# Moving the rank product of the expert routing from between the query parts to behind the second chunk's scores and first values

## The chip, the cores and the metric

The kernel runs on one core of one Trainium2 chip. The metric is the time of the whole kernel on the device in microseconds, the median of several executions. The engines of the core are called by the profile's names: PE (TensorE, matrix products), PEld (its weight loads), DVE (VectorE), ACT (ScalarE), POOL (GpSimd) and SP (SyncE, which issues most DMAs). Each engine works through its own instructions in program order and waits on semaphores of the others.

## The reference: what is computed

One transformer block on x of 8 batches x 2048 tokens x 256 features, all in float32.

```
h = layernorm(x) * (1 + ca) + sa
x = x + ga * attention(h)          # linear attention with decay, 16 heads of 64
h = layernorm(x) * (1 + cb) + sb
x = x + gb * experts(h)            # 8 experts of 256x256, the best 2 for each token
```

Attention: q and k pass through elu + 1, a decay a = sigmoid(h Wa + ba + 2) per head and token multiplies the running state S and the running key sum z, and the output of a token is q S / (q z). Experts: scores by a 256x8 product, softmax, the two best experts with weights of at least 0.1, scaled to sum to one; the output is half of the weighted sum of the two experts' products.

## The kernel before

**Tiling.** The tokens are cut into 64 groups of 256 tokens (8 groups for each batch), and each group into two chunks of 128 tokens. One pass of the main loop (variable n, -2 to 64) works on several groups at once, as a pipeline written out by hand: `here` is group n, whose attention is computed chunk by chunk (objects c0 and c1); `prev` is group n-1, whose attention is done and which is normalised again and routed to experts; `ahead` is group n+1, whose keys, queries and key sums are made; `coming` is group n+2, whose normalised rows are turned and whose decays are made. Expert products of an earlier batch (tiles of 128 rows, `expert_tiles`) are strewn among these steps.

**Order.** The order of the instructions on each engine is the order of the Python statements (`manual_schedule`); nothing reorders them later. Steps that belong to different groups are Python generators, and `advance(gen)` issues the next part of one.

**The routing.** `routing(prev, unit)` (called `rt` in the loop) has six parts, parted by `yield`. Part 1: the gate product and the scores (L642 to L670). Part 2: softmax and the best expert (L672 to L687). Part 3: the second best, `both` (which experts each token uses, L704) and the running count of tokens per expert `hist` (L709, L713). Part 4, the one that is moved: two PE products into the PSUM tile `prank` (L719 with the triangular matrix `before`, L722 with `ones`) give each token its rank among the tokens of its expert; then four DVE instructions make row numbers of it: L729 adds the first row of the expert's list (`rmark`), L734 multiplies the choices with it (`rpicks`), L735 sums them into `places`, and L737 casts them to the integer tile `rrows`. Part 5: four scatters on POOL's queue (L770, a memset of one element, and L771, an indirect DMA that writes 128 rows of `prev` to the lists in DRAM at the rows in `rrows`). Part 6: the weights (`weigh`, L659 to L662 on DVE). Each of the parts 1 to 6 is issued by one `advance(rt)` in a pass.

The last two groups (62 and 63) are not routed through lists (`DenseUnit`): for them part 4 issues nothing. So part 4 works in 62 passes, n = 1 to 62, and in all of them `here` exists.

**Around the old place of part 4.** `qp = project(ahead.hT, "q", ...)` makes the queries in four parts. A part is 8 matmuls on PE into a tile `pq` (L340), two activations on ACT into `lowq` (L350, L351; two buffers) and one DVE instruction that writes `qT` (L352). After each part, POOL multiplies the key sums by it (`times_queries`, L1177). Part 4 of the routing stands behind the second part's `times_queries(1)` and ahead of the third part of the queries: on PE its products lie between the second and the third `pq`, and on DVE its four instructions lie between the second and the third `qT`.

**Around the new place.** After the queries come, for the second chunk of `here`: `c1.scores(0)` (L506 on PE, two products by DVE, L515), `c1.keys()` (transposes L525 on PE, DVE writes `kd`, L528; not for the last group of a batch), `c1.scores(1)` (L506, L515), and `c1.values(0)` (4 matmuls `pv` on PE, L542, a copy on ACT, L549). Then come part 5, the scatters; `expert_tiles` (L884 turns a tile's rows into `pxt`, L900 multiplies them into `py`, L904 on DVE adds the bias into `yg`); the statistics of another group's rows (L283, L284); `denominators` (PE sums `pd`, L463, from what POOL's L1177 left; DVE makes the reciprocal `rd`, L471 and L472, which goes out to DRAM and comes back spread as `rb`); `c1.values(1)`; part 6 of the routing; `decayed_queries` (POOL, L1062); and the second chunk's outputs (`po`, L562 and L579 on PE; DVE's L591 multiplies them by `rb`).

**PSUM.** Tiles of 2 KB rotate through two rings of four. The ring "mm" holds `pq`, `pk`, `pv`, `pxt`, `py` and `pw`; the ring "big" holds the scores `sc` (four in a chunk), `po`, `ps`, the small tiles of the routing (`prank` among them) and `pd`. A tile can be written when the tile four places before it in its ring has been read.

Of the kernel before, what the change touches and what calls it, by code (L numbers as in the profile page):

```python
# [30 lines left out]
def adaln_block_kernel(  # L31
# [1019 lines left out]
    def advance(gen, k=1):  # L1051

        for _ in range(k):
            if gen is not None:
                next(gen, None)
# [66 lines left out]
    def expert_tiles(k=1, look=True):  # L1122
        while queue and not queue[0].unit.dense and on_chip() < AHEAD:
            load_tile()
        if queue and not loaded:
            load_tile()
        for i in range(k):

            while loaded and len(turned) < (2 if look or i + 1 < k else 1):
                t = loaded.pop(0)  # L1130
                t.turn()
                turned.append(t)
            if turned:
                now = turned.pop(0)
                now.apply()
                load_tile()
                left[now.unit.n] -= 1
                if left[now.unit.n] == 0:
                    u = now.unit
                    waiting.extend(Combine(u, g) for g in range(u.first, u.end))  # L1140
                    if u.dense:
                        u.finish()
# [30 lines left out]
    def times_queries(jj):  # L1173

        if ahead:
            part = slice(2 * jj, 2 * jj + 2)
            nc.gpsimd.tensor_mul(zz[:, part, :], zz[:, part, :], ahead.qT[:, part, :])  # L1177

    c0 = plan = planned = None
    for n in range(-2, total + 1):  # L1180
        here, ahead, coming = live.get(n), live.get(n + 1), live.get(n + 2)
# [79 lines left out]
        if prev:  # L1261
# [21 lines left out]
            rt = routing(prev, unit)  # L1283
# [37 lines left out]
        times_queries(0)  # L1321
        advance(qp)
        times_queries(1)
        advance(rt)
        advance(qp)
        keep_sums(slice(4, 8))
        times_queries(2)
# [13 lines left out]
        if here:  # L1341
            c1.scores(0)
            c1.keys()
            c1.scores(1)
        if here:
            c1.values(0)
        advance(rt)
        expert_tiles(share[3])
        advance(dk)
# [110 lines left out]
```

## Time and profile before

| what | value |
|---|---|
| median of 3 executions | 3779.65 us (3770.18 to 3783.37) |
| the profiled execution, its own time | 3800.69 us |
| its span, first to last instruction | 3799.0 us |
| mean granted TensorE clock | 0.974 |
| PE busy | 3545.7 us, 93% of the span |
| DVE busy | 2756.5 us, 73% |
| ACT busy | 2073.6 us, 55% |
| POOL busy | 1891.9 us, 50% |
| part 4's DVE instruction L734, 62 times | 1280 / 1293 / 2054 ns (min / median / max) |

Most passes of the main loop take 50 to 62 us, some of the last ones up to 75 us (by the starts of part 4 in successive passes). A busy share is an average over stages with different limits: which engine sets the pace of a stage is read from the chain of waits and from who waits for whom in that stage.

### The profile page before, as it was taken

The numbers are of one execution on the slowest core, as the hardware profiler recorded it, in microseconds if no ns is written. First come the engines' busy times: TensorE is split into PE (matmuls) and PEld (weight loads), VectorE is DVE, ScalarE is ACT, GpSimd is POOL, SyncE is SP. The second block draws the span as 40 slices with busy tenths as digits, with TensorE's granted clock in tenths as the row PEclk, the third lists the DMA queues.
The fourth block names the chain that finished last, engine by engine and source line by source line (L and its number), as shares of the span: only waits on it lengthen the run. The fifth ranks groups of instructions, "written<-read, shape, count | busy, mean of one in ns | idle before, by whom it ended". The sixth has DMA issues, their size and how long they took to land.

```text
span 3799.0 us, 82207 instructions
## 1 busy us (share of the span) xinstructions
PE 3545.7 (93%) x28998; PEld 2724.2 (72%) x28998; DVE 2756.5 (73%) x6395; ACT 2073.6 (55%) x5295; POOL 1891.9 (50%) x2114
## 2 busy tenths in 40 slices
PE   8999999999999999999999999999999999989876
PEld 6777767777677777777777777777767777767664
DVE  5777788777767777677768668767677677767655
ACT  5555556655555555555546555556555556555532
POOL 2444444343655455454654456454464454555654
PEclk9999999999999999999999999999999999999987
DMA  6555556675676567676575675775775766787866
GB/s 168 142 152 144 141 167 181 185 203 158 192 215 179 179 189 211 177 215 173 173 230 161 200 209 166 206 209 162 200 209 172 202 180 177 216 227 214 229 198 190
DMA packets 347406, 712.11 MB, mean 187 GB/s; under 512 B 43736, under 2 KB 212968, under 8 KB 322416
## 3 DMA queue, kind: packets, MB, share of 16 engines
q1 hardware_dynamic: 318880, 631.29, 59.2%
q0 software_dynamic: 27264, 74.49, 5.8%
q8 instruction: 229, 3.75, 0.4%
q14 instruction: 185, 1.52, 0.1%
q10 hardware_dynamic: 848, 1.07, 0.1%
HBM read 577.29 MB, written 132.53 MB: 187 GB/s over the span
## 4 chain that ended last, share of the span: by engine, by line
PE 62%; DVE 18%; DMA 7%; issue 7%; ACT 3%; POOL 1%; SPq 1%; another core or an unknown queue 0%; DVEq 0%; POOLq 0%
PE pk L340 9%; PE pw L629 9%; PE pv L542 8%; PE py L900 6%; PE po L579 6%; PE pq L340 5%; DVE at L447 5%; PE sc L506 3%; PE ps L613 3%; PE po L562 3%; DVE qT L352 2%; DMA xg<-xrows 2%; PE pxt L884 2%; DVE dec L515 2%; PE pd L463 2%
## 5 line engine op out<-in xcount | busy, mean ns | idle before, releaser
L429 ACT ACTIVATE dec<-dec,lt 128x128 f32<-128x128 f32 x2048 | 629.7, 390 | 20.5 <-POOL dec L423 20.5
L1177 POOL TENSOR_TENSOR at<-at,qT 128x512 f32<-128x512 f32 x256 | 342.2, 1349 | 422.0 <-DVE qT L352 341.0
L340 PE MATMUL pk<-hT_a,wk_sb 128*128 128x256 f32 x2048 | 516.0, 398 | 1.9 <-issue 1.9
L542 PE MATMUL pv<-wv_sb,hT_a 128*128 128x512 f32 x1024 | 486.1, 607 | 11.2 <-DVE qT L352 11.2
L340 PE MATMUL pq<-hT_a,wq_sb 128*128 128x256 f32 x2048 | 489.7, 388 | 1.9 <-DVE yg L904 1.3
L889 ACT ACTIVATE xgT<-pxt,modT,modT 128x128 f32<-128x128 f32 x622 | 249.0, 453 | 427.5 <-PE pxt L884 412.0
L629 PE MATMUL pw<-wo_sb,oT 128*128 128x256 f32 x2048 | 474.6, 385 | 6.4 <-DMA xt<-in_L_attn_x_dram 5.9
L629 PEld LDWEIGHTS pw<-wo_sb,oT 128*128 128x128 f32 x2048 | 389.8, 194 | 60.6 <-DVE oT L591 8.3
L340 PEld LDWEIGHTS pk<-hT_a,wk_sb 128*128 128x128 f32 x2048 | 384.8, 197 | 67.1 <-issue 7.6
L340 PEld LDWEIGHTS pq<-hT_a,wq_sb 128*128 128x128 f32 x2048 | 381.4, 191 | 56.6 <-DVE kT L352 1.7
L447 DVE TENSOR_TENSOR_SCAN at<-at,z,kT 128x256 f32<-128x256 f32 x448 | 396.8, 925 | 2.0
L591 DVE TENSOR_TENSOR oT<-po,rb 128x512 f32<-128x512 f32 x256 | 168.0, 684 | 314.0 <-DMA rb<-rdd 90.0
L423 POOL TENSOR_SCALAR_AFFINE_SELECT dec<-dec 128x2048 f32<-128x2048 f32 x128 | 258.7, 2021 | 273.3 <-DMA dec<-led 218.1
L579 PE MATMUL po<-dec,v 128*64 128x128 f32 x4096 | 299.3, 280 | 68.7 <-issue 63.3
L900 PE MATMUL py<-we,xgT 128*128 128x256 f32 x1244 | 341.4, 399 | 20.6 <-DVE kT L352 8.5
L515 DVE TENSOR_TENSOR dec<-sc,dec 128x512 f32<-128x512 f32 x512 | 326.8, 680 | 42.3 <-PE sc L506 40.0
L542 PEld LDWEIGHTS pv<-wv_sb,hT_a 128*128 128x128 f32 x1024 | 182.9, 190 | 204.7 <-issue 150.6
L579 PEld LDWEIGHTS po<-dec,v 128*64 128x64 f32 x4096 | 235.3, 138 | 127.5 <-issue 109.0
L634 POOL TENSOR_TENSOR xt<-xt,dx 128x256 f32<-128x256 f32 x128 | 93.8, 733 | 446.7 <-DVE dx L633 444.9
L506 PE MATMUL sc<-qT,kT 64*128 64x128 f32 x4096 | 297.3, 285 | 0.0
L506 PEld LDWEIGHTS sc<-qT,kT 64*128 64x128 f32 x4096 | 249.7, 188 | 62.9 <-issue 62.9
L1062 POOL TENSOR_TENSOR el<-el,qT 128x1024 f32<-128x1024 f32 x120 | 285.8, 2381 | 5.6 <-POOL whole L1070 0.2
(198 smaller groups left out, 6155.8 us busy)
## 6 DMA issues: line engine op xcount, KB each, us to landing
dec<-led SPq DMA_DIRECT2D x128, 1024.0 KB
we<-ew_d SPq DMA_DIRECT2D x311, 384.0 KB
at<-ad SPq DMA_DIRECT2D x128, 512.0 KB
el<-led SPq DMA_DIRECT2D x256, 256.0 KB
rb<-rdd SPq DMA_DIRECT2D x128, 512.0 KB
xg<-xrows SPq DMA_DIRECT2D x311, 128.0 KB
yrows<-yg SPq DMA_DIRECT2D x311, 128.0 KB
xt<-in_L_attn_x_dram SPq DMA_DIRECT2D x64, 256.0 KB
```

The source lines that it names most:

```text
L340: nc.tensor.matmul(pp[:, j * GT : (j + 1) * GT], w[:, k, (jj + j) * P : (jj + j + 1) * P], hT[:, k, :], start=(k == 0), stop=(k == KD - 1),)
L423: nc.gpsimd.affine_select(out=dec, in_=dec, compare_op=ALU.is_ge, fill=1e30, base=0, pattern=[[0, H], [1, C]], channel_multiplier=-1,)
L429: nc.scalar.activation(dec[:, h, :], dec[:, h, :], AF.Exp, scale=-1.0, bias=x.lt[:, 0, ch, h : h + 1])
L447: nc.vector.tensor_tensor_scan(zz[:, j, :], at[:, j, :], kT[:, j, :], 0.0 if z is None else z[:, j : j + 1], ALU.mult, ALU.add,)
L506: nc.tensor.matmul(sc[q][:, i, :], self.kT[rows, half * 4 + i, self.tok], self.qT[rows, half * 4 + i, self.tok], start=True, stop=True,)
L515: nc.vector.tensor_mul(w4, sc[q], w4)
L542: nc.tensor.matmul(pv, self.hT[:, k, self.tok], wv_sb[:, k, i * 512 : (i + 1) * 512], start=(k == 0), stop=(k == KD - 1),)
L579: nc.tensor.matmul(po[half * DH : (half + 1) * DH, i, :], self.v[:, h * DH : (h + 1) * DH], self.dec[:, q * NP + j, :], start=(self.S is N ...
L629: nc.tensor.matmul(pw[:, :D], self.oT[:, j, :], wo_sb[:, j, :], start=(j == 0), stop=(j == NP - 1))
L900: nc.tensor.matmul(py[:, :D], self.xT[:, k, :], self.w[:, k, :], start=(k == 0), stop=(k == KD - 1))
L1062: nc.gpsimd.tensor_mul(el, el, x.qT[:, :, ch * C : (ch + 1) * C])
L1177: nc.gpsimd.tensor_mul(zz[:, part, :], zz[:, part, :], ahead.qT[:, part, :])
```

## The change

The fourth `advance(rt)` of a pass moves: it is no longer issued between the second and the third part of the queries when `here` exists, but behind `c1.scores(1)` and `c1.values(0)`, directly ahead of the `advance(rt)` that issues the scatters. In passes without `here` it stays where it was. The two `if here:` blocks become one, which by itself changes nothing.

```diff
         times_queries(0)
         advance(qp)
         times_queries(1)
-        advance(rt)
+        if not here:
+            advance(rt)
         advance(qp)
         keep_sums(slice(4, 8))
         times_queries(2)
...
             c1.scores(0)
             c1.keys()
             c1.scores(1)
-        if here:
             c1.values(0)
+            advance(rt)
         advance(rt)
         expert_tiles(share[3])
         advance(dk)
```

## The prediction

> **What bounds the kernel now.** I read the page first, then the chain of waits over the pass in which part 4 runs at 1610 us (one of the common kind), then the timelines of DVE, ACT and POOL there, then the three lines of PE that this stage's DVE and POOL work releases. The page's span, PE row and chain:
>
> ```profile
> span 3799.0 us, 82207 instructions
> PE 3545.7 (93%) x28998; PEld 2724.2 (72%) x28998; DVE 2756.5 (73%) x6395; ACT 2073.6 (55%) x5295; POOL 1891.9 (50%) x2114
> PE 62%; DVE 18%; DMA 7%; issue 7%; ACT 3%; POOL 1%; SPq 1%; another core or an unknown queue 0%; DVEq 0%; POOLq 0%
> ```
>
> PE is nearly always at work, so a change pays only where it removes or adds a wait of PE. But 18% of the chain is DVE's. Where, the chain of that pass says (start, us, what):
>
> ```profile
> 1605.95 0.14 PE prank L719 x2
> ...
> 1609.86 0.60 DVE qT L352
> 1610.46 0.09 DVE rmark L729
> ...
> 1610.57 1.30 DVE rpicks L734
> ...
> 1612.81 0.38 DVE qT L352
> ...
> 1614.69 0.61 DVE kd L528
> 1615.30 0.04 issue
> 1615.34 1.13 PE py L900 x4
> ```
>
> The chain leaves PE behind the rank product, runs through DVE's scan, the second `qT`, part 4 itself (L729 to L737), the last `qT`, the chunk's masks and `kd`, and comes back to PE only at `py`, which needs the PSUM buffer that `kd` frees. Counted over the windows of the whole chain, it passes L734 in 46 of the 62 passes, with 60.0 us there, and with L729, L735 and L737 beside it 75.0 us. So part 4 lies on the path now. Its DVE instructions in that pass:
>
> ```profile
> 1610.38 0.16 DVE L729 TENSOR_TENSOR rmark<-prank,first_row 128x16 f32<-128x16 f32 x1
> 1610.57 1.29 DVE L734 TENSOR_TENSOR rpicks<-rpicks,rmark 128x32 f32<-128x32 f32 x1
> 1611.90 0.19 DVE L735 TENSOR_REDUCE places<-rpicks 128x4 f32<-128x32 f32 x1
> 1612.12 0.17 DVE L737 CAST rrows<-places 128x4 int32<-128x4 f32 x1
> 1612.21 1.29 DVE L352 SCALAR_TENSOR_TENSOR qT<-pq,lowq 128x512 f32<-128x512 f32 x2
> ```
>
> and what POOL does in the same time:
>
> ```profile
> 1610.54 1.28 POOL L1177 TENSOR_TENSOR at<-at,qT 128x512 f32<-128x512 f32 x1 [1.41 <-DVE rmark L729]
> 1613.05 2.52 POOL L1177 TENSOR_TENSOR at<-at,qT 128x512 f32<-128x512 f32 x2 [1.09 <-DVE qT L352]
> ```
>
> L734 works on 32 elements a partition, like L735 (0.19), yet takes 1.29: it ends when POOL's product, which started 0.03 us before it, ends. This is in every pass:
>
> ```profile
> L734 DVE TENSOR_TENSOR rpicks<-rpicks,rmark x62: 1280/1293/2054, 131.7 to 3618.8; 128x32 f32<-128x32 f32 x62
> ```
>
> Last, who on PE waits for this stage. From the answers for lines L542, L900 and L463, the rows that name its work (us of idle, times; weight loads and matmuls of one wait are both counted):
>
> ```profile
>   DVE qT L352: 26.0, 37
> ```
>
> ```profile
>   DVE kd L528: 20.2, 69
> ```
>
> ```profile
>   POOL at L1177: 9.2, 11
>   POOL mark L770: 8.1, 15
> ```
>
> **The change part by part.** (a) *PE's two products move.* 4 matmul and 4 weight-load instructions a pass, the same number as before. In the old place they take 0.36 us between the two `pq` groups; in the new one they stand behind `pv`. Same PE time, 62 x 0.36 = 22 us taken out here and put in there: net 0. Their old waits for L704 and `hist` (3.3 + 0.6 us by `rpicks`' own answer) fall away; the input is 8 us old at the new place. I count 1 us of that, since most of it lies beside matmuls still in flight.
>
> (b) *DVE's four instructions leave the query parts.* From L729's start to L737's end is 1610.38 to 1612.29 = 1.91 us. The third `qT` can then start at 1610.38 rather than 1612.21, 1.83 us sooner: its `lowq` was ready at 1609.42 (ACT's L351 at 1608.79, 0.63 long). The fourth cannot gain as much: its `lowq` is ready at 1611.81 (L351 at 1611.18, 0.63), since ACT needs the buffer that the second `qT` frees. It starts at about 1611.87 rather than 1612.81: 0.94 us sooner, and all DVE work behind it too, up to the new place (two L515, two L528, two L515), and POOL's last L1177. Nothing of that work is held back by PE: the scores stand on PE 2 us ahead.
>
> (c) *What PE gets of it.* `pv` waits for the third `qT` (gains 1.83), `py` for `kd` (0.94), `pd` for POOL's last L1177 (0.94). Their waits are shorter than these gains (under 0.3 us a time for `kd`, 0.4 to 1.2 for `qT`), so they should vanish. The rows count a wait at the load and at the matmul; half of 26.0 + 20.2 + 9.2 + 8.1 = 63.5 gives 31.8 us. The lower bound is nothing, if these waits come back at the next place; the upper one is the chain's 75.0 us for part 4. I take 31, near the rows of PE's own idle time, because the chain's figure ignores that PE's natural pace is only some tenths behind.
>
> (d) *The four instructions in their new place.* DVE reaches them behind the last L515, at 1617.08 - 0.94 = 1616.14. PE's product is there by then: `pv` starts at 1612.98, less the 0.36 that left PE, plus 1.9 for `pv` and 0.5 for the product: 1615.0, a margin of 1.1 us. POOL has no product running: its L1177s end 0.94 sooner than 1615.57, and then it waits for `rrows`. So L734 should fall to about L735's 0.19 and the four take some 0.8 us: DVE reaches `yg` at about the old time (1616.94 against 1617.00). What is queued behind them (yg, the statistics, `rd`) is not late: 0. Without that margin DVE would stand at L729 with `rd` behind it; that is the second rival.
>
> (e) *POOL's scatters.* The moved part issues no DMA, on no queue; the scatters stay where they are in the program but now wait for `rrows`, at about 1616.9, where the first memset ran at 1615.50: 1.4 us later. Behind them on POOL are the second chunk's `whole` and L1062 (2.36 us). Their reader is the next pass's first `po`, at 1636.8, 12 us after; POOL's next work waits 2.96 us for DVE at that place, so the delay ends there. Where less is idle (1.06 us in early passes), S's decay is 0.3 us later, which PE reads 15 us on. Cost 0. If the cover were gone, 1.4 x 62 = 87 us of POOL time would count. SP is moved past nothing: its next DMA of the stage, `rd`'s, comes at its old time or up to 0.4 us earlier.
>
> (f) *PSUM.* `prank` now takes the buffer of the first score tile rather than one that is long free; that tile is read by the first L515, which ends at 1614.09 - 0.94 = 1613.15, and PE asks for it at 1614.5. `pd` and the `po` tiles shift by one place to tiles read before PE gets to them. 0, with a margin of 1.3 us.
>
> The weights of part 6 now come before L1062 in the passes where L662 waits for it (1053 ns median, 2282 most). The next DVE instruction there waits for PE, so I count nothing.
>
> [...]
>
> **Sum.** -31 (c) - 1 (a) + 0 = -32 us on the profiled execution's own time, 3800.69 (span 3799.0 and 1.7 around it): 3768.7. That execution stands 0.56% above the median of the runs shown, 3779.65; scaled, -32 gives 3748. About 0.3% is what a measurement of this kernel can tell from no change (11 us).
>
> **Rivals.** *It comes back as PE's own issue stalls.* Behind `pd` and `po` PE stands without a semaphore (0.47 us "issue" at 1621.05 in that chain, and longer in the next chunk). If these follow PE's instruction supply rather than the waits ahead, what (c) gains is stood out there: 3775 to 3783, near 3778. For it: the stall comes at the same place in most passes. Against: it is as long in passes that lost 0.5 us more at `pv`, so it does not fill up what is gained.
>
> *The path shortens by DVE's full 0.94 us in the 46 passes where the chain runs through part 4*, since PE's sequencer, freed sooner, also shortens the issue stall: with another 0.5 us in the pv passes, 50 to 60 us: 3725. For it: the chain. Against: PE's idle rows show half.
>
> *Slower: DVE stands at L729 for the product.* PE issues it behind `pv`; if `pv` is late, `yg`, the statistics, `rd` and so `rb` wait with it. It decides where (d)'s margin of 1.1 us is gone; in five of the last seven passes `pv` starts 0.36 to 1.4 us behind the third `qT` and it nearly is. In all passes, with the product 1.1 us behind DVE, `oT` would be later in the 26 where it waits for `rb` (90.0 us in total): 26 x 1.1 = 29 us, 3809. For it: PE gets no faster by this change, while DVE gains 0.94. Against: DVE lags PE by 2 us there in all common passes.
>
> **How the numbers follow.** Forecast as in (c), 3735 to 3765: 0.5. Full path, 3715 to 3735: 0.15. Back as issue stalls, 3768 to 3785: 0.18. Slower, by L729 or by POOL's later queue, 3791 to 3815: 0.17. Faster by over 0.3% takes the first two and a little of the third: 0.67; same 0.16; slower 0.17. The range leaves out half of the slower case and a little at the low end: 3718 to 3797. The likeliest's own range is 3735 to 3765.
>
> **What would show it.** Right: L734 at about 0.2 us in all passes; two or more `qT` back to back behind the second; the rows "DVE qT" at L542 and "DVE kd" at L900 nearly gone; the chain no longer through part 4; the first scatter 1.3 to 1.6 us later against `pv`; L662 at 0.16. Wrong: L729 with idle time before it that PE's `prank` ended; new waits of PE at `pd` or `po`; "issue" time at L579 and L613 up by what the waits lost; L1062 running beside DVE's scans or other instructions, which then take over 1 us.

## The result

The changed kernel takes 3812.74 us (median; 3808.53 to 3824.77), the kernel before beside it on the same chip 3778.44 (3770.18 to 3783.37). The ratio is 1.0095, 95% interval 1.0073 to 1.0118: 34 us slower, where 32 us faster was forecast. The profiled execution of the changed kernel took 3809.48 us; the one of before, 3800.69, stood 0.6% above its median, so the two traces differ by only 9 us.

One thing has to be said ahead, since the numbers below can't be read without it. The later runs came to several chips at several times, and the kernel before itself takes about 3785 us at some of these times and about 3627 at others; chip 3 showed both, 3624 and later 3783. The first pair of runs belongs to the 3785 kind. Every comparison below is with the kernel before on the same chip at the same time, and each says which kind it was: "with the loss" (3778 to 3789) or "without the loss" (3624 to 3629). What is lost will be seen.

The page of the changed kernel (span, busy times, the chain's shares by engine, and the row of the outputs' matmuls: busy us, mean ns, then idle us ahead of them and what ended it):

```profile
span 3807.8 us, 82164 instructions
PE 3544.4 (93%) x28998; PEld 2733.0 (72%) x28998; DVE 2609.0 (69%) x6395; ACT 2077.6 (55%) x5295; POOL 1894.5 (50%) x2114
PE 76%; DVE 9%; issue 6%; DMA 4%; ACT 2%; SPq 1%; POOL 1%; another core or an unknown queue 0%; DVEq 0%; POOLq 0%; ACTq 0%
L579 PE MATMUL po<-dec,v 128*64 128x128 f32 x4096 | 328.8, 282 | 116.6 <-issue 112.4
```

The same row of the page of before:

```profile
L579 PE MATMUL po<-dec,v 128*64 128x128 f32 x4096 | 299.3, 280 | 68.7 <-issue 63.3
```

DVE's share of the chain fell from 18% to 9%: what the change was to take off the path is off it. But the outputs' matmuls, L579, take 29.5 us more of PE's time and stand idle 47.9 us more, together 77 us, and "issue" says that no semaphore held them. The chain over the pass at 1671 us, which is of the same kind as the one shown of before:

```profile
1681.81 1.91 PE pv L542 x4
1683.72 0.13 PE prank L719 x2
...
1688.12 1.03 PE po L562 x32
1689.15 0.91 PE po L579 x13
1690.06 0.32 issue
1690.38 0.34 PE po L579 x2
1690.73 0.43 issue
1691.16 0.44 PE po L579 x4
1691.59 0.99 issue
1692.58 0.93 PE po L579 x13
```

In the old chain DVE's part 4 stood in this place. Now the chain is PE throughout, up to L579, which is cut into pieces by 1.74 us of waiting for nothing that the profile shows. The timeline of the same pass shows DVE, POOL and PE side by side:

```profile
1678.98 1.27 DVE L352 SCALAR_TENSOR_TENSOR qT<-pq,lowq 128x512 f32<-128x512 f32 x2
...
1685.24 0.16 DVE L729 TENSOR_TENSOR rmark<-prank,first_row 128x16 f32<-128x16 f32 x1
1685.44 0.19 DVE L734 TENSOR_TENSOR rpicks<-rpicks,rmark 128x32 f32<-128x32 f32 x1
...
1686.85 1.06 POOL L771 DMA_INDIRECT xrows<-lnn_f,rrows  x1 [3.10 <-ACT dec L429]
...
1689.08 0.98 PE L579 MATMUL po<-dec,v 128*64 128x128 f32 x13
...
1689.50 0.96 POOL L771 DMA_INDIRECT xrows<-lnn_f,rrows  x1 [0.23 <-issue]
...
1690.77 0.96 POOL L771 DMA_INDIRECT xrows<-lnn_f,rrows  x1 [0.22 <-issue]
...
1691.16 0.44 PE L579 MATMUL po<-dec,v 128*64 128x128 f32 x4 [0.43 <-issue]
...
1692.58 0.93 PE L579 MATMUL po<-dec,v 128*64 128x128 f32 x13 [0.99 <-issue]
```

The second and third `qT` run back to back, and L734 takes 0.19. The scatters (L771; the second of the four, at 1688.22, is left out here) start 5.1 us behind `pv` (1681.74), against 2.8 in the pass of before (1615.75 against 1612.98), and so the last three now run on into L579. From 0.6 us behind the start of the third to 0.9 us behind the end of the fourth PE stops three times. The stops are not tied one by one to a scatter's start: over the whole trace they come 0.7 us apart (median), the scatters of a pass 1.3 us.

Over the whole trace PE stands 275 times for more than 0.2 us without a semaphore, 149.8 us in all; before, it was 179 times and 109.5 us.

Over all passes, from the starts of PE's work in the two traces: PE gains 34.8 us from the start of the queries to the second `pv`, and loses 10.3 from the first `po` (L562) to L579 and 89.9 from the second chunk's L579 to its `pw`. At `pk` and the first chunk's outputs, whose instructions the change doesn't touch, the changed kernel's trace is 51 us shorter. How long the 32 matmuls of L579 of one chunk take from the first start to the last, by what POOL does meanwhile: 1.70 us where it is at no indirect DMA, in both kernels (medians); 2.73 in the kernel before where it is at one, and 4.19 in the changed kernel. The matmuls of the scores (L506) take 0.89 us with and without one, those of the values (L542) 1.29 or 1.39 (medians). In the kernel before the scatters ran mostly beside `pd`, the second `pv` and L562, and the gathers (L1004, indirect DMAs too) beside the first chunk's L579 and L613.

### The profile page after: what moved, and what is told of

It is laid out like the page before. It is cut to its first block, busy times and chain, and to the rows that moved or that the text cites. A ratio compares the mean times of both kernels' runs of the same rounds, so it can differ in the third digit from the quotient of the medians.

```text
span 3807.8 us, 82164 instructions
## 1 busy us (share of the span) xinstructions
PE 3544.4 (93%) x28998; PEld 2733.0 (72%) x28998; DVE 2609.0 (69%) x6395; ACT 2077.6 (55%) x5295; POOL 1894.5 (50%) x2114
## 4 chain that ended last, share of the span: by engine, by line
PE 76%; DVE 9%; issue 6%; DMA 4%; ACT 2%; SPq 1%; POOL 1%; another core or an unknown queue 0%; DVEq 0%; POOLq 0%; ACTq 0%
PE pv L542 11%; PE pw L629 10%; PE pk L340 9%; PE pq L340 9%; PE po L579 7%; PE py L900 6%; PE sc L506 6%; PE ps L613 3%; PE po L562 3%; PE pk L525 3%; PE pxt L884 2%; PE pd L463 2%; DVE at L447 2%; DMA xg<-xrows 2%; DVE kT L352 1%
## 5 line engine op out<-in xcount | busy, mean ns | idle before, releaser
L1177 POOL TENSOR_TENSOR at<-at,qT 128x512 f32<-128x512 f32 x256 | 341.8, 1347 | 361.3 <-DVE qT L352 355.6
L340 PE MATMUL pk<-hT_a,wk_sb 128*128 128x256 f32 x2048 | 505.6, 392 | 0.0
L542 PE MATMUL pv<-wv_sb,hT_a 128*128 128x512 f32 x1024 | 486.3, 608 | 0.0
L340 PE MATMUL pq<-hT_a,wq_sb 128*128 128x256 f32 x2048 | 473.1, 384 | 1.5 <-DVE yg L904 1.4
L579 PE MATMUL po<-dec,v 128*64 128x128 f32 x4096 | 328.8, 282 | 116.6 <-issue 112.4
L579 PEld LDWEIGHTS po<-dec,v 128*64 128x64 f32 x4096 | 244.4, 138 | 192.6 <-issue 174.5
L447 DVE TENSOR_TENSOR_SCAN at<-at,z,kT 128x256 f32<-128x256 f32 x448 | 381.0, 890 | 2.0
L515 DVE TENSOR_TENSOR dec<-sc,dec 128x512 f32<-128x512 f32 x512 | 327.5, 682 | 44.0 <-PE sc L506 39.3
L771 POOL DMA_INDIRECT xrows<-lnn_f,rrows x248 | 245.9, 991 | 211.9 <-ACT dec L429 115.0
L900 PE MATMUL py<-we,xgT 128*128 128x256 f32 x1244 | 336.0, 394 | 8.7 <-ACT xgT L889 4.0
L542 PEld LDWEIGHTS pv<-wv_sb,hT_a 128*128 128x128 f32 x1024 | 183.1, 190 | 192.3 <-issue 153.1
L506 PE MATMUL sc<-qT,kT 64*128 64x128 f32 x4096 | 296.3, 285 | 0.0
L506 PEld LDWEIGHTS sc<-qT,kT 64*128 64x128 f32 x4096 | 248.7, 188 | 62.8 <-issue 62.6
```

Of the source, the lines that this page charges most:

```text
L340: nc.tensor.matmul(pp[:, j * GT : (j + 1) * GT], w[:, k, (jj + j) * P : (jj + j + 1) * P], hT[:, k, :], start=(k == 0), stop=(k == KD - 1),)
L447: nc.vector.tensor_tensor_scan(zz[:, j, :], at[:, j, :], kT[:, j, :], 0.0 if z is None else z[:, j : j + 1], ALU.mult, ALU.add,)
L506: nc.tensor.matmul(sc[q][:, i, :], self.kT[rows, half * 4 + i, self.tok], self.qT[rows, half * 4 + i, self.tok], start=True, stop=True,)
L515: nc.vector.tensor_mul(w4, sc[q], w4)
L542: nc.tensor.matmul(pv, self.hT[:, k, self.tok], wv_sb[:, k, i * 512 : (i + 1) * 512], start=(k == 0), stop=(k == KD - 1),)
L579: nc.tensor.matmul(po[half * DH : (half + 1) * DH, i, :], self.v[:, h * DH : (h + 1) * DH], self.dec[:, q * NP + j, :], start=(self.S is N ...
```

## The experiments

**Theory A**: PE's dense short matmuls of the outputs (L579, and L613 for the state) lose time while POOL issues an indirect DMA; the change makes the scatters some 2 us later, out of a stage in which they cost little, into L579; the move of the product itself gains what was forecast. **Rival B**: the loss comes with the product's new place itself, and the scatters have nothing to do with it. Two more reasons came up on the way: **rival C**, that the product's move gains nothing even without the scatters' collision, because what the queries' parts give up comes back in later waits, and **rival D**, that the loss follows from the order of the work and comes at any time.

**The scatters moved alone, product in its old place.** In the routing the weights come ahead of the scatters, and the scatters become a seventh part, issued behind the next group's decayed queries.

```diff
         nc.vector.tensor_copy(rows, unit.places[:, here, :])
         yield
+        yield
+        weigh(unit.weights[:, here, :])
+        yield
         for ch in range(G):
             for n in range(TOP_K):
                 unit.scatter(rows[:, ch, n : n + 1], x.rows[ch])
         yield
-        weigh(unit.weights[:, here, :])
-        yield
...
             decayed_queries(ahead, 0)
+        advance(rt)
         if here:
             c1.from_state()
             c1.outputs(0)
```

> The rank product and its four DVE instructions stay where they were before the change; only the four scatters are issued later on POOL, behind the product of the decayed queries (L1062), with the weights of the routing ahead of them. Theory A (the change lost its time because the scatters, waiting for the row numbers, now run beside the second chunk's outputs, where PE issues some 60 short matmuls in 2 us and stalls while POOL issues an indirect DMA): L579 of the second chunk goes from about 2.8 us to 4 or more in nearly all passes, as in the changed kernel, and the time rises by 1.4 to 2.2 us a pass: 3860 to 3915 us. Theory B (the product itself costs the time at its new place on PE or DVE): no difference to before, 3770 to 3790 us, and L579 stays at 2.8 us.

Measured without the loss (chip 14, before at 3628.85): 3644.6, ratio 1.0035 (1.0017 to 1.0054). In this trace, as in all others of that kind, L579 takes 1.70 us whether or not an indirect DMA runs, so it could not tell the theories apart; it is some 13 us slower even so. The same kernel with the loss:

> The rank product and its DVE work at the old place, only the scatters later, beside the second chunk's L579 and L613. Theory A: on a chip with the stall slower than before by 1.4 to 2.2 us a pass, 1.02 to 1.04 of before, with L579 and L613 of the second chunk at 4 us or more; on a chip without it 1.002 to 1.006 again. Theory B: 0.997 to 1.003 on either.

Measured on chip 7 (before at 3786.83): 3849.97, ratio 1.0165 (1.0123 to 1.0206). Its page (its line numbers behind the edit are one higher: L772 is the scatters' L771):

```profile
PE 67%; DVE 16%; issue 7%; DMA 4%; ACT 3%; SPq 1%; POOL 1%; another core or an unknown queue 0%; DVEq 0%; POOLq 0%; ACTq 0%
L579 PE MATMUL po<-dec,v 128*64 128x128 f32 x4096 | 338.2, 287 | 125.5 <-issue 115.3
```

and its timeline at one pass's second outputs:

```profile
1543.60 1.13 PE L579 MATMUL po<-dec,v 128*64 128x128 f32 x14
1544.24 0.97 POOL L772 DMA_INDIRECT xrows<-lnn_f,rrows  x1 [0.21 <-issue]
1545.14 0.41 PE L579 MATMUL po<-dec,v 128*64 128x128 f32 x3 [0.41 <-issue]
1545.52 0.97 POOL L772 DMA_INDIRECT xrows<-lnn_f,rrows  x1 [0.21 <-issue]
...
1547.32 1.42 PE L579 MATMUL po<-dec,v 128*64 128x128 f32 x12 [0.98 <-issue]
```

The product is where it was (DVE keeps 16% of the chain), and yet L579 shows the changed kernel's row, and 62 us are lost. The second chunk's stretch from L579 to `pw` is 106 us longer than in the trace of before, against 90 in the changed kernel. The scatters start 2.0 us ahead of L579 here and 2.2 in the changed kernel (medians; 4.6 before), so the two kernels differ in little but the product's place and that POOL makes the decayed queries ahead of the scatters here. B falls. A's size does not hold: it expected 1.02 to 1.04, and the measured ratio lies under that.

**The changed kernel again, with the loss.**

> The changed kernel as it is, beside the kernel before on the same chip. Theory A (the loss is PE's stall beside the scatters, which the second chip did not show at all: L579 and L613 at 1.7 and 0.9 us there whether or not an indirect DMA runs): on a chip without that stall (the kernel before near 3630 us) the loss is gone and what is left of the query stage's gain shows, 0.98 to 1.00 of before; on a chip with it (the kernel before near 3780 us) the loss is there again, 1.007 to 1.012 of before, with L579 at 4 us in the second chunk. Theory B (the product costs time at its new place): slower by about 1% on either kind of chip.

Measured on chip 13 (before at 3789.34): 3827.33, ratio 1.0100 (1.0067 to 1.0132). Against the run before this one (chip 7), whose scatters are late too and whose product is in the old place, PE's stages sum to some 31 us less, and the two ratios give 0.9936, or 24 us. So the product's move is worth 24 to 31 us where the scatters are late in both, and the scatters' lateness costs some 62: together the 38 us that this kernel loses on this chip.

**The changed kernel with its scatters at the end of the pass.** The routing's parts as above, and the extra `advance(rt)` behind `c1.project()`.

```diff
         if here:
             c1.project()
+        advance(rt)
         if late:
             fetch_outputs(False)
```

> The rank product at its new place, only the scatters moved to the end of the pass; the gathers stay. Theory A: on a chip with the stall the second chunk's L579 at 1.7 us in nearly all passes and the first chunk's still stalled by the gathers; the 35 us of the query stage and the stall of the kernel before show as 0.975 to 0.99 of before. On a chip without the stall 1.003 to 1.008 again. Theory B (the product's new place costs the time): 1.01 of before, as the changed kernel.

Measured with the loss (chip 7): 3784.0, ratio 0.9996 (0.9974 to 1.0018). The changed kernel's loss of 1% is gone, but the gain that was expected beside it is not there. The second chunk's L579 is whole, 49 us less than before from L579 to `pw`. But the gathers now queue behind the scatters on POOL, and meet the first chunk's L613 and the keys:

```profile
1559.29 1.34 PE L613 MATMUL ps<-v,kd 128*64 128x64 f32 x27
...
1560.77 0.95 POOL L1005 DMA_INDIRECT yc<-yrows,rows  x1 [0.30 <-issue]
...
1562.02 0.95 POOL L1005 DMA_INDIRECT yc<-yrows,rows  x1 [0.30 <-issue]
1562.57 0.22 PE L613 MATMUL ps<-v,kd 128*64 128x64 f32 x1 [1.19 <-issue]
1563.98 0.39 PE L613 MATMUL ps<-v,kd 128*64 128x64 f32 x2 [1.20 <-issue]
```

The 32 matmuls of L613, 0.88 us by themselves, take 2.8 beside an indirect DMA (median of 32 passes). The first DMA of a group (starts under 3 us apart) is not enough: in 19 passes L579 had only that one beside it, as in the pass shown (from 1558.22), and never stopped; and in this trace, those of before, of late scatters and both of the changed kernel with the loss no stop beside a group begins earlier than 1.7 us behind the group's first start. Between the keys' start and the next step (`pa`, L362) PE needs 61 us more than before, and 18 us more ahead of the first chunk's outputs. It is the same thing with other indirect DMAs and other matmuls.

The same kernel, and the kernel before with the scatters in the same place, without the loss (chip 14):

> The rank product at its new place, as in the changed kernel; the scatters leave the stage and are issued at the end of the pass, behind the second chunk's projection, where PE works on long matmuls. Theory A: the second chunk's L579 falls to about 1.8 us, the 35 us that the query stage gained stay, and some 48 us of the stall that was there before the change go as well: 3690 to 3735 us, less if POOL's next select is delayed by the scatters. Theory B: the time stays at the changed kernel's 3813 us.

> The rank product at its old place; the scatters at the end of the pass. Theory A: the second chunk's L579 at about 1.8 us, the query stage as before: some 48 us under the kernel before, 3720 to 3765 us; the difference to the run with the new product and the same scatters is what the move of the product is worth by itself, 25 to 40 us in favour of the move. Theory B: 3770 to 3790 us, and the run with the new product 35 us slower than this one.

Measured: 3648.01, ratio 1.0055 (1.0037 to 1.0073), with the new place of the product, and 3647.83, 1.0054 (1.0022 to 1.0086), with the old one. Both miss what A expected, for the reason given at the first run, and they say that with the scatters at the end the product's move is worth nothing there (a reason is shown further down). The gathers' move alone missed too: `fetch_outputs()` goes behind `decayed_queries(here, 1)`.

```diff
-        if not late:
-            fetch_outputs()
         if here:
             whole_decay(here, 1)
             c1.decay_state()
             decayed_queries(here, 1)
+        if not late:
+            fetch_outputs()
```

> Nothing of the routing moves; the four gathers of expert outputs (L1004, indirect DMAs too) are issued on POOL behind the product of the decayed queries of the second chunk, and not beside the first chunk's outputs. Theory A, that any indirect DMA on POOL beside L579 or L613 stalls PE: the first chunk's L579 and L613, together 4.5 to 5.9 us in passes with gathers, fall to about 2.8 us, and the time by 60 to 120 us: 3660 to 3720 us. If only the scatters do it, or the stalls follow PE's own instruction supply: no difference, 3770 to 3790 us.

Measured: 3640.8, ratio 1.0034 (1.0021 to 1.0047). Without the loss these three kernels win nothing by moving indirect DMAs, and lose 12 to 20 us.

**Which property of the DMAs stalls PE.** Both kernels are the changed one with its scatters at the end, and at the scatters' place four plain DMAs of 128 rows into scratch memory, once on POOL's queue and once on SP's. They wait for the same `rrows`.

```diff
         advance(rt)
+        if prev and here and not unit.dense:
+            nc.gpsimd.tensor_copy(junk_i, prev.rr.rearrange("p c n -> p (c n)"))
+            for ch in range(G):
+                for m in range(TOP_K):
+                    at = (2 * ch + m) * P
+                    nc.gpsimd.memset(mark, 0.0)
+                    nc.gpsimd.dma_start(out=junk_d[at : at + P, :], in_=prev.rows[ch])
         expert_tiles(share[3])
```

> As the run with the new product and the scatters at the end, but at the scatters' place in the changed kernel POOL waits for the row numbers and issues four plain DMAs of the same 128 rows to a scratch area (added work, nothing of the computation left out). If what stalls PE is POOL making DMA descriptors, of whatever DMA: on a chip with the stall L579 of the second chunk goes back to about 4 us. If it is the indirect form alone (POOL reading the row numbers and computing addresses): it stays at 1.7 us.

> The same with SP's queue in place of POOL's: SP waits for the row numbers and issues the four DMAs of 128 KB. If the transfers on the DMA engines stall PE, L579 of the second chunk goes to 3 us or more on a chip with the stall; if it is POOL's part in a DMA, it stays at 1.7 us.

Measured with the loss (chip 7), one execution each: 3779.22 and 3791.41. The timeline of the first:

```profile
1546.40 0.54 POOL L1359 DMA_DIRECT2D junk_d<-lnn_f  x1
...
1547.02 1.97 PE L579 MATMUL po<-dec,v 128*64 128x128 f32 x32
```

and of the second:

```profile
1554.60 1.90 SPq L1358 DMA_DIRECT2D junk_d<-lnn_f  x4
...
1556.11 1.97 PE L579 MATMUL po<-dec,v 128*64 128x128 f32 x32
```

All 32 matmuls of L579 run through (1.97 us to the last end, 1.70 to the last start), and so they do in all 62 passes of both runs. POOL's four take some 0.6 us each to issue, a scatter 0.97, and end just ahead of L579's start; SP's issue runs 0.4 us into it. Of the 192 packets that POOL's four move in a pass some 80 (median) start beside L579, while in the changed kernel, where it stops, its 1.70 us have 8 or 9 packets of POOL's queue beside them. So it is not the moving of four times 128 rows. What of the indirect form it is was not told apart; POOL issuing plain DMAs during L579 itself was not tried.

**All indirect DMAs away from the outputs.** Scatters at the end and gathers behind the decayed queries, with the new and the old place of the product, with the loss (chips 13 and 3):

> The product at its new place, the scatters at the end of the pass and the four gathers behind the product of the decayed queries, so that no indirect DMA runs beside either chunk's outputs. Theory A: on a chip with the stall 80 to 150 us faster than before (0.96 to 0.98), with L579 and L613 at 1.7 and 0.9 us; on a chip without it 0.998 to 1.006 of before, as the runs that moved only the scatters or only the gathers there. Theory B: 1% slower on either.

> The kernel before with the scatters at the end of the pass and the gathers behind the second chunk's decayed queries, once more, for a chip that shows the loss (the kernel before at about 3780 us). Theory A: 0.970 to 0.985 there, against 0.9735 for the same places with the product moved (measured on such a chip). On a chip without the loss: 0.999 to 1.003.

Measured: 3686.53 against 3789.34, ratio 0.9735 (0.9697 to 0.9772), with the new place, and 3696.61 against 3782.99, ratio 0.9766 (0.9746 to 0.9785), with the old one. They beat the kernel before by 103 and 86 us, and the first of them beats the changed kernel on its chip by 141. The row of the second, from the groups of instructions:

```profile
L579 PE MATMUL po<-dec,v 128*64 128x128 f32 x4096 | 265.1, 281 | 16.1 <-issue 11.8
```

L579 gives back 87 us against the row of before, and L613 has no idle time left. This is A's clearest case, and it doesn't need the change: the old place of the product gives nearly all of it, and the two intervals overlap.

The same pair without the loss (chip 1 twice, then chip 3), and beside the second of them the changed kernel as it is:

> The kernel before (product and rows among the parts of the queries, as it was), with the scatters at the end of the pass and the gathers behind the second chunk's decayed queries. Theory A (PE's matmuls of L579 and L613 lose time only while POOL issues an indirect DMA): on a chip on which the kernel before takes about 3780 us, no such loss is left in the outputs' rows, L579 about 1.7 us a run of 32 starts, and the time is 0.970 to 0.985 of the kernel before. On a chip on which the kernel before takes about 3630 us there is nothing to lose: 1.002 to 1.008. Rival B (the new place of the product causes the loss by itself): as without the change, 0.997 to 1.003.

> The same places of the scatters and gathers with the product and the rows where the change puts them. Theory A with the forecast's sum (PE gets 32 us from the move once no indirect DMA is beside the outputs): 20 to 40 us less than the old product with the same places, about 0.965 to 0.978 of the kernel before on a chip on which that takes 3780 us. Rival C (the move gains nothing even then, since what the queries' parts give up comes back in later waits of the same pass): within 6 us of the old product with the same places.

> The changed kernel as it is, beside the next two on the same chip. Theory A (PE's matmuls of L579 and L613 lose time while POOL issues an indirect DMA, and the change puts the scatters beside L579): on a chip on which the kernel before takes about 3780 us and its runs of 32 starts of L579 beside an indirect DMA take 2.7 us or more, 1.007 to 1.013; on a chip on which the kernel before takes about 3630 us and those runs take 1.7 us, the loss is not there, 0.992 to 1.006. Rival D (the loss is a matter of the order of the work alone and comes on every chip): 1.007 to 1.013 there too.

> The kernel before with the scatters at the end of the pass and the gathers behind the second chunk's decayed queries, the product where it was. Theory A: 0.970 to 0.985 on a chip with the loss, 0.999 to 1.003 on one without. Rival D: 0.999 to 1.003 on both.

> The same with the product and the rows where the change puts them. By the forecast's sum (32 us gained by the move wherever the scatters cost nothing): 20 to 40 us less than the old product with the same places. By rival C (what the queries' parts give up comes back in later waits): within 15 us of it, on either side.

> The kernel before with the scatters at the end of the pass and the gathers behind the second chunk's decayed queries, for a chip that shows the loss in the outputs' matmuls (the kernel before at about 3780 us). Theory A: 0.970 to 0.985 there. On a chip without the loss: 0.999 to 1.003 again.

> The same with the product and the rows where the change puts them, for the same chip. By the forecast's sum: 20 to 40 us less than the old product with the same places. By rival C: within 15 us of it, on either side, as on the chip without the loss (11 to 16 us more there).

| kernel, without the loss | us | ratio to before | 95% interval |
|---|---|---|---|
| old place, all moved | 3631.17, 3634.48, 3630.4 | 1.0009, 1.0014, 1.0011 | 0.9993 to 1.0029 |
| new place, all moved | 3646.66, 3646.24, 3649.71 | 1.0041, 1.0045, 1.0060 | 1.0022 to 1.0078 |
| the changed kernel | 3618.66 | 0.9981 | 0.9967 to 0.9995 |

(The intervals of the first two rows reach from the lowest bound to the highest of the three.) The changed kernel, slower by 1% with the loss, is faster by 0.2% without it. Its timeline there, at the second outputs of a pass:

```profile
1507.57 0.98 POOL L771 DMA_INDIRECT xrows<-lnn_f,rrows  x1 [0.21 <-issue]
...
1508.10 1.97 PE L579 MATMUL po<-dec,v 128*64 128x128 f32 x32
1508.85 0.97 POOL L771 DMA_INDIRECT xrows<-lnn_f,rrows  x1 [0.22 <-issue]
...
1509.89 1.10 PE L613 MATMUL ps<-v,kd 128*64 128x64 f32 x32
1510.13 0.97 POOL L771 DMA_INDIRECT xrows<-lnn_f,rrows  x1 [0.22 <-issue]
```

The scatters lie beside L579 and L613 as they do in the trace with the loss, and take as long, but PE runs through: in this whole trace it stands once for more than 0.2 us without a semaphore, where the trace with the loss has 275. D falls: the order is the same and the loss is not. The groups' row of the same trace:

```profile
L579 PE MATMUL po<-dec,v 128*64 128x128 f32 x4096 | 255.6, 277 | 1.2 <-DVE dec L515 0.3 <-ACT v L549 0.2
```

Where all indirect DMAs are moved, the product's move gains nothing, as C says: 12 to 19 us slower without the loss (past C's own bounds of 6 and 15 us in two of the three pairs), and 0.3% faster with it, within the two intervals. But another reason than C's shows, and it makes these pairs no measure of the change. From the run with the new place on chip 3, without the loss, the row of L734, and DVE and POOL in one pass (L1063 is L1062 of before):

```profile
L734 DVE TENSOR_TENSOR rpicks<-rpicks,rmark 128x32 f32<-128x32 f32 x62 | 53.0, 855 | 2.1
```

```profile
1524.40 2.37 POOL L1063 TENSOR_TENSOR el<-el,qT 128x1024 f32<-128x1024 f32 x1
...
1525.87 0.94 DVE L734 TENSOR_TENSOR rpicks<-rpicks,rmark 128x32 f32<-128x32 f32 x1
```

L734 takes 855 ns again, in the mean, not the 229 that it has in the changed kernel with the loss (without the loss 0.19 us, in that kernel's pass shown, at 1504.80). With the scatters at the end, POOL no longer waits for `rrows` at this place but starts the product of the decayed queries at once, and L734 ends when that ends: in 54 of 62 passes here, and in 50 to 55 passes of each of five other runs with the new place and the scatters at the end. In the run where POOL's four plain DMAs wait for `rrows` at this place it takes 0.19 again (median). Besides, PE's wait for `hT_a` at L362 is 92.4 to 104.6 us with the new place and 64.2 to 70.3 with the old; the changed kernel, which is faster than both, has 86.3, so that wait does not set the time by itself.

A fairer pair, with the scatters equally late, is the changed kernel and the run with the scatters moved alone, both without the loss: 0.9981 against 1.0035, some 20 us for the product's move (two chips, each against its own kernel before). There C falls.

## Why the prediction was wrong

**(a), (b), (d), (f): as forecast.** PE's products stand behind `pv` without a wait worth naming; the third `qT` runs behind the second; L734 fell from 83.8 to 14.2 us in all (1352 to 229 ns mean); the product was done at 1684.08 and DVE came to L729 at 1685.24, a margin of 1.2 us for 1.1 forecast; the new row for PSUM at `prank` (13.1 us until L515) is idle time of weight loads, and the products themselves stand 0.2 us in all. The rival in which DVE stands at L729 for the product did not come. The runs with the scatters at the end show what (d) rested on: POOL waiting for `rrows` there.

**(c): right.** The rows of `qT` at L542 (26.0) and of `kd` at L900 (20.2) are gone. Of POOL's two rows at L463 this is left:

```profile
  POOL at L1177: 4.6, 5
  POOL mark L770: 1.6, 3
```

63.5 us became 6.2; half of the difference is 28.7, for 31 forecast. L542 has a new row in the changed kernel,

```profile
  DVE rrows L737: 11.5, 28
```

which stands where the row of `yg` (13.7, 35) stood: the moved instructions are now the last ahead of the second `pv`, and cost no more there. From the queries to the second `pv`, PE gains 34.8 us against the trace of before; between two kernels with equally late scatters 24 with the loss and 30 without it. By the ratios of such pairs it is 24 and 20 us, so the term may be somewhat too large, but it is not what failed.

**(e): the step that failed.** "Their reader is the next pass's first `po` ... the delay ends there. Cost 0": the delay was followed through what reads the scatters' result and through what queues behind them on POOL, and the next pass's first outputs were indeed no later: PE's stretch from that chunk's first scores to its L579 is 551.0 us in all before and 551.2 after. It was not asked what runs beside the scatters. The delay was also 2.3 us in the pass shown, not 1.4: `rrows` was there when forecast, and the first scatter started 0.8 us after it. At the new time they fall on L579, and the price is 62 us by the run that makes only the scatters late (47 to 78 by its interval), for a term of 0. -32 + 62 = +30 against +34 measured. The bound that the text gives, 87 us, has the right size for a wrong reason: it is POOL's time, and it was PE's that was lost. "Slower, by L729 or by POOL's later queue, 3791 to 3815" holds the measured time by luck: neither of its two reasons came.

The trace of before had the sign: 63.3 us of "issue" at L579, 27.1 at L613,

```profile
L613 PE MATMUL ps<-v,kd 128*64 128x64 f32 x3840 | 158.2, 229 | 27.1 <-issue 27.1
```

and of these stalls all but one (167 of 168) end within 2 us of the start of an indirect DMA. **The first rival** came nearest. It named "issue" stalls behind `pd` and `po`, at 0.47 us in the chain shown, and asked whether they would give the gain back. Its condition was PE's instruction supply; it was not compared with what POOL was doing at those moments, which would have shown that the change moves four indirect DMAs a pass into the stretch with the stalls. The supply itself is not borne out: packets of the instruction queues, 427 of some 0.8 us with the loss and without, run beside 39 of the 179 stalls of over 0.2 us before and 50 of the 275 after, a fifth where chance alone would give a sixth. "Issue" at L579 rose by 49 us (at L613 it fell by 8.5), and the last line of "what would show it" had that as the sign of failure.

**The scatters' own time.** Each of the 248 scatters takes as long in the changed kernel as before: 991 ns in the mean (957 to 1197), 989 before (956 to 1194). They are late, not longer. With the loss, L579's 1.70 and 4.19 us (medians, without and beside an indirect DMA of POOL) say that PE can lose time beside one; what holds it there no run here shows, and without the loss L579 takes 1.70 us either way.

**What stays open.** What makes the loss come and go, on one chip, at two times. The granted clock is not it: 0.974 and 0.977 with the loss and 0.986 without differ by 1.2%, at most 46 us if all the time went by it, and the traces place the 150 us in the stalls' stages: 53 us from L579 to `pw` and 100 in the first chunk's outputs between the trace of before and that of the changed kernel without the loss. One lead is in the trace itself. The same program (the old place with all moved; chip 1, then chip 3) left 42,948 records of DMA landings without the loss and 37,170 with it (32,422 and 32,537 are in the traces of before and of the changed kernel, with the loss too), while the records of DMA packets are complete in both (347,418 and 347,419). They are not missing evenly: of those in the first 6 us from the start of each group of indirect DMAs 57% are missing (2455 against 5724), in the next 14 us 11% (23,492 against 26,365). So with the loss records go missing above all while indirect DMAs run. If PE stopped where it leaves most records, L562 and L613 would stop first: PE leaves 64 of weight loads and matmuls at L562 in 0.84 us, 64 at L613 in 0.88 and 64 at L579 in 1.70, one behind the other, where the scores have 32 in 0.89. That fits in part only: L562 is the fastest and hardly stops (4.4 us of "issue" in the changed kernel, where L579 has 112.4), and L579 by itself leaves no more a microsecond than the scores. Whether the missing records and the stops have a cause in common no run here shows. If the recording has a part in the stops, the loss belongs to it and not to the kernel; an execution that leaves no records would tell.

Nor is it settled what the late scatters cost without the loss, where they stop nothing. There the change gains 7 us rather than 32, and the record splits this in two: some 20 for the product's move, as above, less some 13 that the late scatters cost (1.0035, the first run). No trace of the kernel before of that kind shows where the 13 lie. Against its nearest relative that has one (the old place with all moved, chip 1), the changed kernel is 22 us faster up to the second `pv` and gives back 11 in the rest of the pass.

## What to carry to other kernels

When a step that starts DMAs gets later, ask not only who reads them and who queues behind them, but what will run beside them then; here four indirect DMAs of POOL, 2 us later, cost some 62 us with the loss, more than the 24 to 31 that the move had gained. "Issue" time at one line and not at others of the same engine is a question to the trace: set the stalls' times beside the starts on the other engines before you call them PE's own. A control that moves a second part out of the way can bring back what the change took off: with the scatters at the end L734 met another product of POOL, and took 855 ns in the mean instead of 229. And when the kernel before differs by 4% from one time to another, no single comparison tells the sign of a change: this one is 1% slower in one surrounding and 0.2% faster in another.

## What the runs showed of the hardware

Where the loss is there, 32 short matmuls in a row (L579: weights of 128x64, 128 columns, 1.70 us) take 2.7 to 4.3 us (medians) while POOL issues indirect DMAs, and L613's 32 (weights of 128x64 too, 64 columns, 0.88 us) 2.8 to 3.7, without a wait for a semaphore; the stops begin 1.7 us or more behind the first DMA of a group. The scores (L506, 16 matmuls in 0.89 us) and the values (L542, 4 of 512 columns in 1.29 or 1.39) take the same beside them (medians). Four plain DMAs of SP issued beside L579, or of POOL just ahead of it, leave it whole (1.70 us in all 62 passes, one execution of each). Without the loss, with the same indirect DMAs beside the same matmuls, L579 takes 1.70 us, PE stands once for more than 0.2 us without a semaphore in the changed kernel's whole trace, and the kernel before takes 3627 us where it took 3785. A DVE instruction on 32 elements a partition (L734), 0.19 us by itself, takes 1.29 beside POOL's L1177 and 0.94 beside its L1062 (medians), and ends with them (in 57 of 62 passes before, in 54 of 62 in the run shown).
